# Two 16-head attentions: the diagonal corrections directly behind their scores, and two PSUM evictions per batch on ACT

## The chip, the cores and the metric

The kernel runs on one core of a Trainium2 chip. The metric is the time of one execution on the device in microseconds; a kernel's time is the median of its runs. A profile is one further execution, recorded by the hardware profiler. Names in it: PE is TensorE (matmuls), PEld its weight loads, DVE is VectorE, ACT is ScalarE, POOL is GpSimd, SP is SyncE, which issues DMAs here.

## The reference, cut to what matters

Four blocks follow each other on `x` of shape (8, 512, 128), each with a residual addition and a LayerNorm: an attention (layer 0), a feed-forward with FP4 quantization, a second attention (layer 1), and two layers of local attention with a feed-forward. The change touches the two 16-head attentions alone. Layer 0's adds a bias to the scores that falls with the distance of query and key (ALiBi); layer 1's has none.

```python
slopes = jnp.power(2.0, 8.0 * jnp.arange(0, -H, -1, dtype=jnp.float32) / H)
qkv = x @ W_qkv.T + b_qkv                       # B=8, S=512, H=16 heads of 8
...
scores = jnp.einsum('bhqd,bhkd->bhqk', q, k) / math.sqrt(Hd)
rel = jnp.abs(pos[None, :] - pos[:, None]).astype(jnp.float32)
bias = -slopes[:, None, None] * rel             # layer 0 only
probs = jax.nn.softmax(scores + bias[None], axis=-1)
out = jnp.einsum('bhqk,bhkd->bhqd', probs, v)
...
return out @ W_out.T + b_out
```

## The kernel before, in words

**Two passes over the scores.** `attention` (from L121) forms each head's scores twice. The first pass (`s_ps`) has queries on the partitions and 512 keys along the row, and DVE takes each row's maximum from it (L239). The second pass (`t_ps`) has keys on the partitions and 512 queries along the row; its operands hold one row more, the maximum found before, so that it yields the scores already shifted. ACT turns them into exponentials `e` (L245), which PE multiplies with the values (`values`, tile `av`). A column of ones among the values gives the denominators.

**Corrections.** Layer 0's bias comes from extra rows in the products' operands. They give the right distance everywhere but in the two 64 x 64 blocks on the diagonal that belong to the 128 partitions of a tile. `corrected` (L199) repairs these with four small bf16 products per pair of tiles, `sel` as weights and `tri` as the moving operand, 64 columns each, accumulated into the same tile. Layer 1 has `alibi` False and no corrections.

**Units and steps.** A unit is a batch and a group of four heads, 32 units per layer, eight steps each. `step(u, i, v, k)` (L209) does the first pass of two heads for unit `u` and 128 queries, and the second pass of two heads for unit `v`, which is two units (`LAG` of 16 steps) behind. The two heads of a step lie on the upper and the lower half of the array's rows (`slice(64 * j, ...)`), so their products can run side by side. A layer has 256 steps with scores and 256 with shifted scores, 16 steps later.

**What sets the order.** The order on PE is written out by hand: `mm` and `tr` (L126, L127) keep the program's order, so that nearly all PE rows of the profile bear these two lines; they are told apart by their tiles. Between steps, `todo` inserts the rest at fixed steps (L306 to L331): the transposition of the maxima (`shift`, tile `m_ps`, behind odd steps), the value products (behind even steps), the division (`divide`, `o_ps`), and once per batch `begin_x` (transposed input, `xt_ps` to `xT`), two `begin_qk`, `begin_v`, `end_o` (transposed output, `ot_ps` to `oT`) and `end_y`. DVE, ACT and POOL run in the order that the planner gives them from the same program.

**Buffers.** PSUM's eight banks are split into three for `s_ps` (two are used per step), four that `t_ps` shares with every other product (`bank`), and one for `av`.

```python
p_s, p_t, p_av = pool("as", 3, space=PSUM), pool("at", 4, space=PSUM), pool("aav", 1, space=PSUM)
```

Of the kernel before, what the change touches and what calls it, by code (L numbers as in the profile page):

```python
# [40 lines left out]
def body(ctx, tc, x, consts, rows, wa0, wa1, acols, bo, wf, wqkv, wo, w1, w2, cols, b2r, qs, ks, out):  # L41
    nc = tc.nc
# [78 lines left out]
    def attention(li, alibi, qs_, ks_, late=None):  # L121
# [6 lines left out]
        with ExitStack() as st:  # L128
# [21 lines left out]
            def begin_x(b, h):  # L150
                ps = bank("xt_ps")
                for c in range(NT):
                    tr(ps[:, c * P : (c + 1) * P], xn[:, b * NT + c, :], ident)
                h["xT"] = work.tile([P, S], F32, tag="xT", name="xT", bufs=1)
                nc.vector.tensor_copy(h["xT"], ps)

            def begin_qk(b, h, n):
                ps = bank("qk_ps")
# [40 lines left out]
            def corrected(ps, lo, at, stop):  # L199

                for a in range(2):
                    for j in range(2):
                        r = slice(64 * j, 64 * j + 64)
                        mm(
                            ps[j][:, lo + 64 * a : lo + 64 * a + 64], lhsT=sel[r, a * P : (a + 1) * P],
                            rhs=tri[r, at : at + 64], start=False, stop=stop and a == 1, skip_group_check=True,
                        )

            def step(u, i, v, k):  # L209


                if u:
                    blk, pp = i // 2, i % 2
                    p, lo = 2 * u["g"] + pp, (i // 2) * P
                    q, kk = qs_[u["b"] % 2], ks_[u["b"] % 2]
                    ps = [p_s.tile([P, S], F32, tag="s", name="s_ps") for j in range(2)]
                    for j in range(2):
                        r = slice(64 * j, 64 * j + 63)
                        mm(
                            ps[j], lhsT=q[r, p, lo : lo + P], rhs=kk[r, p, :], start=True, stop=not alibi,  # L220
                            skip_group_check=True,
                        )
                if v:
                    vp, vlo = 2 * v["g"] + k % 2, (k // 2) * P
                    q, kk = qs_[v["b"] % 2], ks_[v["b"] % 2]
                    ts = [bank("t_ps") for j in range(2)]
                    for j in range(2):
                        r = slice(64 * j, 64 * j + 64)
                        mm(
                            ts[j], lhsT=kk[r, vp, vlo : vlo + P], rhs=q[r, vp, :], start=True, stop=not alibi,  # L230
                            skip_group_check=True,
                        )
                if u:
                    if alibi:
                        corrected(ps, lo, 0, True)
                    if i == 0:
                        u["m"] = work.tile([P, 2, 2, NT], F32, tag="m", name="m")
                    for j in range(2):
                        nc.vector.tensor_reduce(u["m"][:, j, pp, blk : blk + 1], ps[j], AX.X, ALU.max)  # L239
                if v:  # L240
                    if alibi:
                        corrected(ts, vlo, 64, True)
                    for j in range(2):
                        e = work.tile([P, S], F32, tag="e", name="e", bufs=13)
                        nc.scalar.activation(e, ts[j], AF.Exp, scale=float(SLOPES[2 * vp + j]) if alibi else 1.0)  # L245
                        v["e"].append(e)
# [43 lines left out]
            def end_o(h):  # L290
                ps = bank("ot_ps")
                for c in range(NT):
                    tr(ps[:, c * P : (c + 1) * P], h["o"][:, c, :], ident)
                h["oT"] = work.tile([P, S], F32, tag="oT", name="oT", bufs=1)
                nc.vector.tensor_copy(h["oT"], ps)

            def end_y(b, h):
                ps = bank("y_ps").rearrange("p (c d) -> p c d", c=NT)
# [11 lines left out]
            for n in range(B * G):  # L310
                b, g = divmod(n, G)
                units.append({"b": b, "g": g, "h": batch[b], "e": []})
                s, z = n * NU, n * NU + LAG
                later(s + 9, shift, units[n])
                later(z + 12, divide, units[n])
                for blk in range(NT):
                    later(z + 2 * blk + 4, values, units[n], blk)
                if g == 0 and b + 1 < B:

                    early = max(s - 10, 1)  # L320
                    later(early, begin_x, b + 1, batch[b + 1])
                    later(early + 2, begin_qk, b + 1, batch[b + 1], 0)
                    later(early + 4, begin_qk, b + 1, batch[b + 1], 1)
                    for part in range(2):
                        for j in range(2):
                            later(s + 6 + 12 * part + 2 * j, load_qk, b + 1, batch[b + 1], j, part)
                    later(s + 20, begin_v, b + 1, batch[b + 1])
                    later(s + 20, with_bias, b + 1)
                if g == G - 1:
                    later(z + 15, end_o, batch[b])  # L330
                    later(z + 18, end_y, b, batch[b])  # L331

            begin_x(0, batch[0])
            begin_qk(0, batch[0], 0)
            begin_qk(0, batch[0], 1)
# [4 lines left out]
            ps = bank("c_ps")[:, 0:P]  # L340
# [5 lines left out]
            for s in range(B * G * NU + LAG + 20):  # L346
                n, i = divmod(s, NU)
                m, k = divmod(s - LAG, NU)
                step(units[n] if n < B * G else None, i, units[m] if 0 <= m < B * G else None, k)
                for f, a in todo.pop(s, []):  # L350
                    f(*a)
# [562 lines left out]
```

## Time and profile before

| | us |
|---|---|
| median of three runs (2224.75 to 2230.90) | 2230.73 |
| the profiled execution's own time | 2234.28 |
| span of the profile, first to last instruction | 2232.5 |
| PE / PEld busy | 1784.9 / 985.4 |
| DVE busy | 1483.3 |
| ACT busy | 1156.5 |
| POOL busy | 830.6 |

Layer 0's attention lies at about 58 to 570 us of the span, the quantized feed-forward until about 763, layer 1's attention until about 1240, the rest belongs to the last block. A row of the page's fifth part reads: line, engine, operation, tile written, tile read, shape, count | busy us in total, mean ns of one | idle us of the engine just before such instructions, and what ended most of that idle time. In the timeline a line is: start in us, length in us, engine, line, operation, tiles, shape, count, and in brackets the idle time before it and its releaser. Several instructions of one kind close together are merged into one line.

### The profile page before, as it was taken

Reading aid. Unit: us, or ns where it says so; the run is one execution under the profiler, and the core shown is the slowest. Engines: PE = TensorE matmul, PEld = TensorE weight load, DVE = VectorE, ACT = ScalarE, POOL = GpSimd, SP = SyncE. Lnnn points to the kernel's source line nnn. Section 1 sums busy time; section 2 is a strip of 40 time slices with the busy share of each in tenths; the row PEclk is TensorE's granted clock in tenths of the full one; section 3 lists DMA queues with packets and bytes.
Section 4 is the critical chain, followed back from the end, with each engine's and each line's share of the span. In section 5 each row is a group of like instructions: output and inputs, shape, how many; then the busy total and the mean of one; then the engine's idle time right before and its main releaser. Section 6 shows DMA issues by size and latency. Waiting matters only on the chain.

```text
span 2232.5 us, 38302 instructions
## 1 busy us (share of the span) xinstructions
PE 1784.9 (80%) x14215; PEld 985.4 (44%) x14245; DVE 1483.3 (66%) x3156; ACT 1156.5 (52%) x2717; POOL 830.6 (37%) x880
## 2 busy tenths in 40 slices
PE   1899999999466589999999568788888888888884
PEld 0444444444244333333333235455555555555553
DVE  2677777776788368888886367566666666666662
ACT  0266666667222237777777145455555555555561
POOL 2302222212545521222211445444444444555554
PEclk6699999999678669999999779899999999999997
DMA  6522223210000132223210011111111111111110
GB/s 115 156 54 59 54 49 53 59 21 2 11 1 0 30 95 58 58 60 64 63 37 2 24 24 29 27 27 25 27 27 27 26 27 26 29 29 30 27 35 19
DMA packets 91627, 88.44 MB, mean 40 GB/s; under 512 B 45825, under 2 KB 57473, under 8 KB 91442
## 3 DMA queue, kind: packets, MB, share of 16 engines
q1 hardware_dynamic: 86752, 85.00, 17.3%
q8 instruction: 113, 1.85, 0.4%
q0 software_dynamic: 4096, 0.54, 0.2%
q14 instruction: 72, 0.59, 0.1%
q10 hardware_dynamic: 594, 0.47, 0.1%
HBM read 41.33 MB, written 18.87 MB: 27 GB/s over the span
## 4 chain that ended last, share of the span: by engine, by line
PE 29%; DVE 17%; ACT 13%; POOL 4%; issue 1%; DMA 1%; SPq 0%; ACTq 0%; POOLq 0%; DVEq 0%
ACT pw L463 7%; PE s_ps L126 6%; PE av L126 5%; PE qk_ps L461 4%; DVE t L564 3%; DVE r L560 3%; DVE m L239 3%; DVE ss L568 3%; DVE m L624 3%; ACT sq L463 2%; PE t_ps L126 2%; PE p_ps L462 2%; PE gp L461 1%; PE ap L461 1%; ACT L463 1%
## 5 line engine op out<-in xcount | busy, mean ns | idle before, releaser
L239 DVE TENSOR_REDUCE m<-s_ps 128x1 f32<-128x512 f32 x1024 | 647.4, 684 | 229.5 <-PE s_ps L126 120.6
L245 ACT ACTIVATE e<-t_ps 128x512 f32<-128x512 f32 x1024 | 552.9, 595 | 240.7 <-PE t_ps L126 236.1
L126 PE MATMUL s_ps<-k,q 63*128 63x512 f32 x1024 | 384.7, 511 | 108.5 <-DVE m L239 65.6
L126 PEld LDWEIGHTS s_ps<-k,q 63*128 63x128 f32 x1024 | 151.6, 192 | 401.3 <-DVE m L239 288.3
L463 ACT ACTIVATE pw<-sp,m,nrm 128x128 f32<-128x128 f32 x512 | 226.5, 461 | 153.0 <-DVE m L626 140.5
L126 PE MATMUL t_ps<-q,k 64*128 64x512 f32 x1024 | 286.2, 426 | 0.3 <-ACT e L245 0.2
L126 PE MATMUL av<-e,va 128*32 128x512 f32 x2048 | 275.2, 608 | 0.0
L257 POOL DMA_DIRECT2D q<-mt x128 | 68.4, 538 | 505.4 <-ACT mt L253 505.4
L571 POOL TENSOR_TENSOR r<-r,t 128x1024 f32<-128x1024 f32 x64 | 151.1, 2360 | 231.0 <-DVE t L564 221.6
L560 DVE TENSOR_TENSOR r<-qk_ps,tab 128x512 f32<-128x512 f32 x128 | 87.7, 685 | 160.6 <-ACT sq L463 160.6
L461 PE MATMUL qk_ps<-wqkv_s,hT 128*128 128x512 f32 x256 | 151.1, 721 | 45.8 <-ACT hT L464 30.3
L637 POOL TENSOR_TENSOR pw<-pw,den 128x1024 f32<-128x1024 f32 x64 | 121.4, 1897 | 137.4 <-DVE den L636 137.3
L126 PEld LDWEIGHTS t_ps<-q,k 64*128 64x128 f32 x1024 | 127.2, 188 | 16.7 <-ACT e L245 16.5
L463 ACT ACTIVATE sq<-qk_ps 128x1024 f32<-128x1024 f32 x64 | 67.2, 1050 | 94.9 <-PE qk_ps L461 89.7
L463 ACT ACTIVATION_READ_ACCUMULATOR pw<-sp,m,nrm 128x1 f32 x512 | 106.0, 207 | 0.0
L462 PE MATMUL p_ps<-cst,pw 128*128 128x128 f32 x512 | 77.9, 290 | 29.9 <-DVE pT L668 11.0
L668 DVE COPY pT<-p_ps 128x512 f32<-128x512 f32 x128 | 83.9, 686 | 23.7 <-PE p_ps L462 22.1
L461 PE MATMUL gp<-nT,w_s 128*128 128x512 f32 (+1 forms) x96 | 61.0, 722 | 45.4 <-ACT u L463 45.3
L462 PE MATMUL t_ps<-cst,r 128*128 128x128 f32 x512 | 78.2, 296 | 22.9 <-DVE xs L702 19.9
L564 DVE TENSOR_TENSOR t<-qk_ps,tab 128x256 f32<-128x256 f32 x256 | 95.3, 413 | 0.0
L461 PEld LDWEIGHTS qk_ps<-wqkv_s,hT 128*128 128x128 f32 x256 | 51.1, 222 | 95.0 <-issue 59.2
L126 PEld LDWEIGHTS <-sel 64*128 64x128 bf16 x2048 | 69.3, 97 | 52.1 <-issue 39.2
(161 smaller groups left out, 3208.5 us busy)
## 6 DMA issues: line engine op xcount, KB each, us to landing
far<-parts SPq DMA_DIRECT2D x64, 256.0 KB
q<-far SPq DMA_DIRECT2D x256, 64.0 KB
k<-far SPq DMA_DIRECT2D x256, 64.0 KB
ve<-v SPq DMA_DIRECT2D x112, 128.0 KB
xn<-in_x SPq DMA_DIRECT2D x8, 256.0 KB
q<-mt POOLq DMA_DIRECT2D x128, 4.0 KB, 2.9
hn<-xs SPq DMA_DIRECT2D x16, 128.0 KB
out<-xn SPq DMA_DIRECT2D x8, 256.0 KB
```

The source lines that it names most:

```text
L126: mm = lambda *a, **k: tc.keep_in_program_order(nc.tensor.matmul(*a, **k))
L239: nc.vector.tensor_reduce(u["m"][:, j, pp, blk : blk + 1], ps[j], AX.X, ALU.max)
L245: nc.scalar.activation(e, ts[j], AF.Exp, scale=float(SLOPES[2 * vp + j]) if alibi else 1.0)
L257: nc.gpsimd.dma_start(out=q[at : at + 1, 2 * g : 2 * g + 2, :].bitcast(F32).rearrange("o a (c t) -> o (a c) t", t=P), in_=mt[8 * j : 8 * j ...
L461: mm = lambda *a, **k: tc.keep_in_program_order(nc.tensor.matmul(*a, **k))
L462: tr = lambda *a, **k: tc.keep_in_program_order(nc.tensor.transpose(*a, **k))
L463: act = lambda *a, **k: tc.keep_in_program_order(nc.scalar.activation(*a, **k))
L560: nc.vector.tensor_tensor(heads(r[:, n]), heads(ps[:, n]), cos.unsqueeze(1).broadcast_to([P, HEADS, DH]), ALU.mult)
L564: nc.vector.tensor_tensor(heads(t2[:, n])[:, :, a : a + 32], heads(ps[:, n])[:, :, 32 - a : 64 - a], sin[:, a : a + 32].unsqueeze(1).broad ...
L571: nc.gpsimd.tensor_tensor(r, r, t2, ALU.add)
L637: nc.gpsimd.tensor_tensor(pw.rearrange("p s r k -> p (s r) k"), pw.rearrange("p s r k -> p (s r) k"), den.rearrange("p s r -> p (s r)").un ...
L668: nc.vector.tensor_copy(h["pT"][:, s], ps)
```

## The change

In `step`, the four corrections of the first pass are issued directly behind the two score products and ahead of the two shifted-score products; before, they stood behind those. The corrections of the second pass stay where they were. In `begin_x` and `end_o` the copies out of PSUM into `xT` and `oT` move from DVE to ACT: one each per batch and layer, 32 in all. On ACT each of them takes its place behind the exponentials of the step after which it is called.

```diff
@@ begin_x
                 h["xT"] = work.tile([P, S], F32, tag="xT", name="xT", bufs=1)
-                nc.vector.tensor_copy(h["xT"], ps)
+                nc.scalar.copy(h["xT"], ps)
@@ step
                             ps[j], lhsT=q[r, p, lo : lo + P], rhs=kk[r, p, :], start=True, stop=not alibi,
                             skip_group_check=True,
                         )
+                    if alibi:
+                        corrected(ps, lo, 0, True)
                 if v:
...
                 if u:
-                    if alibi:
-                        corrected(ps, lo, 0, True)
                     if i == 0:
                         u["m"] = work.tile([P, 2, 2, NT], F32, tag="m", name="m")
@@ end_o
                 h["oT"] = work.tile([P, S], F32, tag="oT", name="oT", bufs=1)
-                nc.vector.tensor_copy(h["oT"], ps)
+                nc.scalar.copy(h["oT"], ps)
```

## The prediction

> **What bounds the kernel now.** I read the page first, then the stretches of equal work, then the waits, then single steps in the timeline. The page puts the two attention layers' row of maxima at the top:
>
> ```profile
> L239 DVE TENSOR_REDUCE m<-s_ps 128x1 f32<-128x512 f32 x1024 | 647.4, 684 | 229.5 <-PE s_ps L126 120.6
> ```
>
> It is not saturated, though. In the stretch of layer 0 in which the granted clock is whole (98.9 to 546.8 us; columns: PE, PEld, DVE, ACT, POOL, clock, DMA share, GB/s) DVE is busy 335 of 448 us and ACT 289:
>
> ```profile
> 98.90:546.80 447.90, 411.71 (x4115) 203.71 (x4115) 335.48 (x604) 289.13 (x555) 91.83 (x128) 1.00 0.22 44
> ```
>
> So a loop of waits sets the pace. The waits from 160 to 540 us name it (total, times, longest): scores wait for a maximum, and the maximum waits for PE, in fact for the shifted scores' products.
>
> ```profile
> PEld s_ps L126 <- DVE m L239: 112.0, 156, 0.8
> ...
> DVE m L239 <- PE t_ps L126: 88.3, 187, 1.7
> ```
>
> In layer 1 (850 to 1160 us), which has no corrections, the same maximum waits for its own scores:
>
> ```profile
> DVE m L239 <- PE s_ps L126: 50.1, 85, 1.6
> ```
>
> The timeline of two steps of layer 0 shows the loop (start, length, engine, what):
>
> ```profile
> 301.80 0.50 PE L126 MATMUL s_ps<-k,q 63*128 63x512 f32 x2
> ...
> 302.14 0.40 PE L126 MATMUL t_ps<-q,k 64*128 64x512 f32 x2
> ...
> 302.38 0.23 PE L126 MATMUL s_ps<-tri,sel 64*128 64x64 bf16 x4
> 302.44 0.22 PE L126 MATMUL t_ps<-tri,sel 64*128 64x64 bf16 x4
> ...
> 302.65 1.29 DVE L239 TENSOR_REDUCE m<-s_ps 128x1 f32<-128x512 f32 x2 [0.54 <-PE t_ps L126]
> ...
> 303.40 0.50 PE L126 MATMUL s_ps<-k,q 63*128 63x512 f32 x1 [0.42 <-DVE m L239]
> ...
> 303.98 0.23 PE L126 MATMUL s_ps<-tri,sel 64*128 64x64 bf16 x2
> ...
> 304.20 1.06 PE L126 MATMUL av<-e,va 128*32 128x512 f32 x8
> 304.23 1.29 DVE L239 TENSOR_REDUCE m<-s_ps 128x1 f32<-128x512 f32 x2 [0.28 <-PE t_ps L126]
> ...
> 305.20 0.49 PE L126 MATMUL s_ps<-k,q 63*128 63x512 f32 x2
> ```
>
> Call the step at 301.80 X (odd) and the next Y (even, followed by the value products av). With three s_ps buffers and two per step, Y's second score needs the first maximum of X.
> - X to Y, 1.60 us, hangs on DVE: 0.58 until the first correction, 0.27 until the maximum starts, 0.69 for it, 0.06 until the score starts (303.40).
> - Y to the next X, 1.80 us, hangs on PE alone: score, shifted score, corrections, then av until 305.20. DVE's maximum that the next X needs would be done at 304.23 + 0.69 = 304.92.
>
> A pair takes 3.40 us.
>
> **What the Trainium skill says.** "TensorE: Matmul & The Clock Gate", section "Step-by-step: what each phase is for": a weight load is pulled ahead of running matmuls when the background weight buffer is free. The trace agrees: behind the long score, t_ps takes 0.24 us to its successor (302.14 to 302.38), while the score, whose load was held by the wait, takes 0.34. The same page, "Weight-path perf modes — Fast Weight Load (FWL) and DoubleRow", has faster loads for 128 weights that are not FP32: the trace has 97 ns for sel against 188 to 192 for t_ps and s_ps. Its section "The mechanism" says that matmuls start and end in program order. Starts here don't (a t_ps correction at 303.88, ahead of the s_ps ones at 303.98), but the maximum at 304.23 waited for the later, so ends are counted in order. "SBUF — State Buffer", "Who interferes with whom": ACT never waits for another engine's port; ACT's 0.59 us copy at 770.58 beside a busy POOL agrees.
>
> **Part 1: corrections behind their scores (layer 0 only).** Nothing is added or removed: four small products per step change places with the two shifted scores. No DMA moves, and POOL's and SP's orders stay as they were.
>
> *Gain, X to Y.* The corrections start 0.34 after the score instead of 0.58. The maximum starts at 0.34 + 0.27 = 0.61 instead of 0.85, Y's score at 0.61 + 0.69 + 0.06 = 1.36 instead of 1.60: 0.24 us saved. Layer 1 supports it: with no corrections its scores start at 1002.88, its maximum at 1003.41 while the t_ps products run, and its Y score at 1004.16, 1.28 later. PE has time: its own work in X would let Y begin at 0.70 to 0.80.
>
> *Loss.* t_ps now follows a short correction, so its weight load is no longer hidden. Layer 0's tail, where steps have no scores, shows that very order:
>
> ```profile
> 541.16 0.39 PE L126 MATMUL t_ps<-q,k 64*128 64x512 f32 x2
> 541.39 0.23 PE L126 MATMUL s_ps<-tri,sel 64*128 64x64 bf16 x4
> 541.46 0.22 PE L126 MATMUL t_ps<-tri,sel 64*128 64x64 bf16 x4
> 541.51 0.48 PE L126 MATMUL t_ps<-q,k 64*128 64x512 f32 x2
> 541.84 0.23 PE L126 MATMUL t_ps<-tri,sel 64*128 64x64 bf16 x4
> ```
>
> t_ps behind a score has 0.23 to 0.24 to its successor, behind a correction 0.33: 0.09 more. In X it falls into PE's wait for DVE (0.80 against 1.36) and costs nothing; if that cover went, it would be another 0.09. In Y it lies on the path: 1.80 becomes 1.89. Its bounds are 0 (the load hidden after all) and 0.24 (as much as the gain, if turning to and fro between bf16 and f32 costs more than the tail shows); I take 0.09.
>
> *Sum.* A plain pair gains 0.24 - 0.09 = 0.15. From step 21 (97.4 us, clock whole) to 254 there are 117 pairs. Seven hold ot_ps in X (0.59 us more of PE, 285.27 to 285.86): there PE reaches Y at 0.80 + 0.67 = 1.47, so 0.1 is saved and 0.09 lost, nothing. 110 x 0.15 = 16.5. Steps 16 to 20 are at half clock and PE-bound: 5 x 0.1 = 0.5 lost. The 16 steps before have no t_ps, the 16 behind no scores. Layer 0: **16.0 us**.
>
> ACT's exponentials come later by the 0.09 and sooner with the pair; ACT would be busy (289 + 8) of 432 us, 69% instead of 65%. Y's second t_ps needs, in steps with m_ps or ot_ps, the bank of X's first exponential: free at about 1.09 + 0.60 + 0.06 = 1.75, wanted at 1.36 + 0.41 = 1.77. That cover is thin, and a miss of 0.05 in the 36 pairs concerned would cost 2 us.
>
> **Part 2: 32 copies of 0.69 us from DVE to ACT, 0.59 there (rows of L193 and L272).** Off DVE in layer 0: xT at 284.58 ends ahead of the maximum at 285.33; oT at 286.53 delays Y's maxima by 0.23, which nobody on PE's path needs. So nothing is gained, but with the maximum due at 0.61 instead of 0.85, xT left on DVE would be late. In layer 1 xT at 1041.64 delays the maximum from 0.53 to 0.72 behind its scores: 6 x 0.15 = **1 us**, the ot_ps products capping it. On ACT, xT lies between Y's and X's exponentials, where ACT idles 1.3 us (285.47, 1042.29); oT lies behind X's and delays Y's by about 0.2, which the av products, using exponentials three steps old, don't feel. If it did hold the banks, it would be 0.2 x 13, under 3 us. At the start of layer 1 the xT copy took 1.69 us on DVE (763.19), beside other DVE and POOL work, and 14 us of loading follow from it; ACT would have it at about 763.9 instead of 764.9: **1 us** (0 to 1.1). Two tails 0.1 each: **0.2**. The first xT of layer 0 starts nothing that is late.
>
> Together 16.0 + 2.2 = **18 us**. The profiled execution took 2234.28 us (span 2232.5), 3.5 above the median of 2230.73; the gain is subtracted from the median: **2212 us**. A measurement of this kernel can tell about 0.3%, 6.7 us.
>
> **Rivals.**
> - *The load is free* (0 instead of 0.09): 0.24 x 110 + 2.2 = 28.6, 2202. Against it: the tail's 0.33. Chance 0.1.
> - *The gain is eaten:* the reload, or banks held by ACT, costs about 0.2 per pair: 110 x 0.04 + 2 = 6, 2224 to 2230. For it: the thin bank margin. Chance 0.11.
> - *Slower:* the maximum does not start sooner, its release still tied to the t_ps pair. Then X to Y grows by 0.09 and Y to X by 0.09: 110 x 0.18 - 2 = +18, 2249. It decides from a maximum starting later than about 0.78 behind its scores (0.85 - 0.09 + the 0.02 of part 2). For it: the page's releaser is t_ps. Against it: layer 1's start at 0.53 with t_ps still running. Chance 0.07.
> - *The order is not as written* (the planner moves the corrections back): the built order has the four corrections between the pairs in every step, so next to no chance.
>
> The forecast keeps 0.71. Range 2202 to 2225, from the free load to most of the gain eaten. Faster by over 0.3% (below 2224): the forecast and the free load, 0.82; within it 0.11, slower 0.07.
>
> **What would show it.** Right: "DVE m <- PE t_ps" gone from the waits, "<- PE s_ps" in its place; maximum 0.61 behind the scores, Y's score 1.36, next X 1.89 later; pair 3.25; t_ps to its correction 0.33; layer 1's step pair still 2.93. Wrong: the maximum at 0.8 or later, Y to X above 2.04 (the whole 0.24 lost), PE waiting for exponentials ahead of t_ps, or DVE gaps behind ACT's copies.

## The result, and the profile after

The changed kernel takes **2208.93 us** (median of four runs, 2201.63 to 2214.46) against 2230.57 (four runs): by the medians 21.6 us less. The ratio of the runs is given as 0.9915 with a 95% interval of 0.9889 to 0.9940, about 19 us (13 to 25); it is not the quotient of the two medians, which is 0.9903. The profiled execution took 2210.63 us with a span of 2208.9; the one before took 2234.28 and 2232.5.

The page's row of the maxima has the same busy time as before and names the scores for nearly all of its idle time, 241.8 us instead of 120.6 (before, another 108.4 of its 229.5 us stood behind the shifted scores' products):

```profile
L239 DVE TENSOR_REDUCE m<-s_ps 128x1 f32<-128x512 f32 x1024 | 647.9, 685 | 247.2 <-PE s_ps L126 241.8
```

The waits of layer 0 from 160 to 520 us say where that comes from (engine and line, what it waited for, us in total, times, longest). The maximum now waits for its own scores' products, and the scores' weight loads wait for the maximum 76 us instead of 112 in the slightly longer window shown before. No wait of a maximum for t_ps is left.

```profile
ACT e L245 <- PE t_ps L126: 87.7, 160, 1.4
DVE m L239 <- PE s_ps L126: 76.8, 104, 1.8
PEld s_ps L126 <- DVE m L239: 76.2, 131, 0.8
```

The timeline of one pair of steps shows why. X has its scores at 259.55, Y its second score at 260.90.

```profile
259.55 0.49 PE L126 MATMUL s_ps<-k,q 63*128 63x512 f32 x2
...
259.89 0.23 PE L126 MATMUL s_ps<-tri,sel 64*128 64x64 bf16 x4
...
259.96 0.48 PE L126 MATMUL t_ps<-q,k 64*128 64x512 f32 x2
260.16 2.63 DVE L239 TENSOR_REDUCE m<-s_ps 128x1 f32<-128x512 f32 x4 [0.71 <-PE s_ps L126]
...
260.28 0.23 PE L126 MATMUL t_ps<-tri,sel 64*128 64x64 bf16 x4
...
260.90 0.18 PEld L126 LDWEIGHTS s_ps<-k,q 63*128 63x128 f32 x1 [0.40 <-DVE m L239]
...
261.80 1.07 PE L126 MATMUL av<-e,va 128*32 128x512 f32 x8
...
262.80 0.50 PE L126 MATMUL s_ps<-k,q 63*128 63x512 f32 x2
```

The maximum starts at 260.16, 0.61 behind the scores and while t_ps is still running. Y's second score follows at 260.90, 1.35 behind them. The next X is at 262.80, another 1.90 later. t_ps has 0.32 us to its correction (259.96 to 260.28). It is so throughout: in the median of the 81 plain ones of layer 0 the maximum starts 0.61 behind the first score, 0.85 before the change, and Y's first score 0.80 behind X's instead of 0.70.

The stretch from step 21 to the last scores, called the steady stretch below, before (97.4 to 540.8) and after, in the columns of the earlier stage line:

```profile
97.40:540.80 443.40, 407.25 (x4070) 202.07 (x4069) 334.29 (x602) 284.92 (x545) 90.69 (x126) 1.00 0.22 45
```

```profile
97.60:525.80 428.20, 421.02 (x4070) 203.78 (x4069) 327.43 (x589) 291.25 (x558) 90.62 (x126) 1.00 0.23 46
```

PE has the same 4070 products, and the stretch is 15.2 us shorter. PE's busy time rises by 13.8 us all the same, so it is no measure of the work here. Thirteen copies have left DVE (602 to 589 instructions) and come to ACT (545 to 558).

Where the time went, from the starts of the first and last scores and of layer 1's first xT copy in each trace:

| stretch, us | before | after |
|---|---|---|
| start to first scores, to step 21 | 36.5 + 60.9 | 37.3 + 60.3 |
| layer 0, step 21 to the last scores | 443.4 | 428.3 |
| to layer 1's xT copy (quantized feed-forward) | 222.4 | 221.1 |
| xT copy to layer 1's first scores | 22.0 | 20.2 |
| to step 21, to the last scores | 36.1 + 393.2 | 35.0 + 392.5 |
| the rest (the last block) | 1018.0 | 1014.3 |

The last block's code is untouched. In all profiles of this study it takes between 1008.2 and 1018.0 us, so its 3.7 us here are not put down to the change. The stretch up to layer 1's xT copy lies between 221.0 and 224.5 in the kernels of this study, and layer 1's first 21 steps take 35.2 us in the corrections-only kernel, whose code for layer 1 is that of the kernel before; so neither of these two differences is shown to be the change's.

### The profile page after: what moved, and what is told of

Read it like the earlier page. It is cut to its first block, busy times and chain, and to the rows that moved or that the text cites. A ratio compares the mean times of both kernels' runs of the same rounds, so it can differ in the third digit from the quotient of the medians.

```text
span 2208.9 us, 38298 instructions
## 1 busy us (share of the span) xinstructions
PE 1788.6 (81%) x14215; PEld 982.2 (44%) x14245; DVE 1467.8 (66%) x3124; ACT 1171.9 (53%) x2749; POOL 829.8 (38%) x880
## 4 chain that ended last, share of the span: by engine, by line
PE 28%; DVE 17%; ACT 13%; POOL 4%; issue 2%; DMA 1%; SPq 0%; ACTq 0%; POOLq 0%; DVEq 0%
ACT pw L463 7%; PE s_ps L126 6%; PE av L126 6%; PE qk_ps L461 4%; DVE t L564 3%; DVE r L560 3%; DVE m L239 3%; DVE ss L568 3%; DVE m L624 2%; ACT sq L463 2%; PE t_ps L126 2%; PE p_ps L462 2%; PE gp L461 1%; PE ap L461 1%; ACT L463 1%
## 5 line engine op out<-in xcount | busy, mean ns | idle before, releaser
L239 DVE TENSOR_REDUCE m<-s_ps 128x1 f32<-128x512 f32 x1024 | 647.9, 685 | 247.2 <-PE s_ps L126 241.8
L126 PE MATMUL s_ps<-k,q 63*128 63x512 f32 x1024 | 373.9, 510 | 78.4 <-DVE m L239 31.8
L126 PE MATMUL t_ps<-q,k 64*128 64x512 f32 x1024 | 301.8, 452 | 0.3 <-ACT e L245 0.2
L126 PEld LDWEIGHTS t_ps<-q,k 64*128 64x128 f32 x1024 | 135.5, 189 | 16.7 <-ACT e L245 16.4
L126 PEld LDWEIGHTS <-sel 64*128 64x128 bf16 x2048 | 83.4, 97 | 72.4 <-issue 41.9
L668 DVE COPY pT<-p_ps 128x512 f32<-128x512 f32 x128 | 84.0, 687 | 21.6 <-PE p_ps L462 19.9
```

The costliest lines, as they stand in the source:

```text
L126: mm = lambda *a, **k: tc.keep_in_program_order(nc.tensor.matmul(*a, **k))
L668: nc.vector.tensor_copy(h["pT"][:, s], ps)
```

## The experiments

Each kernel starts from the changed one, or from the one before, as said. Numbers per pair are medians of the time between the starts of the second scores of successive steps, worked out from the traces, between step 21 and step 254; "X to Y" runs from an odd step to the even one, "Y to X" from there to the next odd step. Of the 117 pairs 29 have the m_ps product behind X and 7 the ot_ps products; the other 81 are the plain ones.

| layer 0, X to Y + Y to X, us | plain | m_ps in X | ot_ps in X | step 21 to last scores |
|---|---|---|---|---|
| before | 1.59 + 1.80 | 1.59 + 1.80 | 1.59 + 2.85 | 443.4 |
| changed | 1.35 + 1.89 | 1.35 + 1.89 | 1.48 + 2.95 | 428.3 |
| corrections only | 1.35 + 1.89 | 1.35 + 1.89 | 1.48 + 2.95 | 428.1 |
| load covered | 1.35 + 2.02 | 1.35 + 2.09 | 1.60 + 3.08 | 446.3 |
| 16 products more in X | 1.35 + 1.89 | 1.35 + 2.09 | 1.70 + 2.94 | 435.1 |
| 16 products more in Y | 1.35 + 2.12 | 1.35 + 2.12 | 1.47 + 3.18 | 455.0 |
| shifted scores first, k = 0, 4, 6 | 1.36 + 1.50 | 1.36 + 1.89 | 2.13 + 2.54 | 398.5 |
| shifted scores first in all even steps | 1.35 + 1.50 | 2.12 + 1.48 | 2.12 + 2.54 | 408.8 |

**Corrections only.** The changed kernel with its copies back on DVE:

```diff
-                nc.scalar.copy(h["xT"], ps)
+                nc.vector.tensor_copy(h["xT"], ps)
...
-                nc.scalar.copy(h["oT"], ps)
+                nc.vector.tensor_copy(h["oT"], ps)
```

> The corrections moved as in the change, the copies into xT and oT left on DVE. Theory (the loop score - maximum - next score is shortened by 0.24 us per pair of steps, a weight load of 0.09 is uncovered): layer 0 keeps nearly all its gain, 14 to 16 us; in the seven pairs with xT the copy now ends after the maximum could start and takes back 0.1 to 0.15 each; layer 1 is as before. Time 2213 to 2217. Rival (the gain comes from relieving DVE of 32 copies of 0.69 us): little or nothing is left, 2226 to 2231.

Measured: 2213.24 us, ratio to before 0.9915 (0.9901 to 0.9929), no different from the whole change. Layer 0 keeps all of its gain. The corrections carry the gain that these times can tell; the rival that the copies carry it falls. One expectation failed: xT on DVE was to take back 0.1 to 0.15 in seven pairs. There are six such pairs in the steady stretch, and it cost 0.10 in one of them and nothing in five. The timeline of one of the five shows the copy in the way and the maximum at 276.82, 0.72 instead of 0.61 behind the scores of 276.10:

```profile
276.21 0.69 DVE L155 COPY xT<-xt_ps 128x512 f32<-128x512 f32 x1 [0.71 <-PE xt_ps L127]
276.82 1.28 DVE L239 TENSOR_REDUCE m<-s_ps 128x1 f32<-128x512 f32 x2
```

But these five X steps also hold the ot_ps products, and PE reaches Y at 1.47 to 1.48 anyway. The sixth, step 23, holds none: there Y follows at 1.45 instead of the changed kernel's 1.35.

**Copies only.** The kernel before with the two copies on ACT (the same lines, the other way round).

> The 32 copies on ACT as in the change, the corrections left where they were. Theory: layer 0's pairs stay at 1.60 + 1.80 us; layer 1 gains about 1 in six pairs with xT and 1 to 2 at its start, where the DVE copy took 1.69 us: 2226 to 2229. Rival (the copies carry the gain): 2209 to 2214. The sum of this run's and the other half's gains should be that of the change, 21.6, within 3.

Measured: 2223.47 us, ratio 0.9973 (0.9959 to 0.9988): by the ratio 6 us less (the medians are 7.6 apart). It lies below the 2226 to 2229 that were expected. Its trace finds 0.4 us in layer 0 (443.0) and 1.0 us in layer 1 from step 21 on (392.2). At layer 1's start the copy of 1.69 us becomes one of 0.58. The first line is the kernel before, the second this one:

```profile
763.19 1.69 DVE L155 COPY xT<-xt_ps 128x512 f32<-128x512 f32 x1
```

```profile
761.89 0.58 ACT L155 COPY xT<-xt_ps 128x512 f32<-128x512 f32 x1 [0.41 <-ACT xn L112]
```

The way from there to the first scores is 19.8 us instead of 22.0, but with the copy on DVE the corrections-only kernel has 20.7, and the kernels with it on ACT lie between 18.3 and 20.4; so about 1 us is put down to the copy, which is shorter by that much, and the rest to the loading's own spread. That leaves 2 to 3 us that the trace can place; for the rest of the 6 it shows no place but the first steps of the layers and the last block, which vary as much without a change. The two halves' gains were to add up to 21.6 within 3. They come to 0.85% and 0.27%, together 1.12% or 25 us, a little over 3 too much and just past the upper end of the whole change's interval (0.60 to 1.11%). The halves' own intervals (0.71 to 0.99% and 0.12 to 0.41%) leave room for a plain sum. But corrections alone and the whole change have the same ratio, so what the copies add in time lies between nothing and some 6 us and is not settled; only the traces place 2 to 3.

**The load covered.** In layer 0 a product with zeros opens each t_ps bank behind the corrections of s_ps, and the shifted scores accumulate onto it (calls set on one line here and below):

```diff
+                    if alibi:
+                        for j in range(2):
+                            r = slice(64 * j, 64 * j + 64)
+                            mm(ts[j], lhsT=sel[r, 0:P], rhs=zero[r], start=True, stop=False, skip_group_check=True)
...
-                            ts[j], lhsT=kk[r, vp, vlo : vlo + P], rhs=q[r, vp, :], start=True, stop=not alibi,
+                            ts[j], lhsT=kk[r, vp, vlo : vlo + P], rhs=q[r, vp, :], start=not alibi, stop=not alibi,
```

> Layer 0 only: a product of sel with zeros, 512 columns, opens each t_ps bank ahead of the shifted scores, which accumulate onto it, so a long bf16 product stands between the corrections and the shifted scores. Theory (the 0.09 us is the weight load of t_ps, uncovered behind a short product): t_ps to its correction falls from 0.33 to 0.24 us; the added product costs 0.22 to 0.24 on the path in Y and nothing in X, so Y to X is about 2.04 and layer 0 is 15 to 20 us longer. Rival (the 0.09 is the price of turning from bf16 to f32 operands): t_ps to its correction stays 0.33, and Y to X is 2.13.

Measured: 2219.91 us in one run; layer 0 is 18.0 us longer than the changed kernel's. The quantity that was named cannot be read: the shifted scores start 0.03 behind the zeros in the trace, so a start there is not the moment at which a product streams.

```profile
262.36 0.38 PE L126 MATMUL t_ps<-zero,sel 64*128 64x512 bf16 x2
262.39 0.58 PE L126 MATMUL t_ps<-q,k 64*128 64x512 f32 x2
262.81 0.23 PE L126 MATMUL t_ps<-tri,sel 64*128 64x64 bf16 x4
```

What can be read is both together: 0.45 us (262.36 to 262.81) for two products of 512 columns. That is twice 0.22 to 0.24. With the 0.33 of an uncovered load 0.12 would be left for the zeros, half of what such a product takes. Y to X is 2.02, as the weight load predicts (2.04), and not 2.13. So the 0.09 fits a load that is hidden by a long product ahead of it and not by a short one; a fixed price for turning from bf16 to f32 is against the sum. The load itself was not measured apart; the reading rests on these sums.

**Sixteen products more in X, or in Y.** Small products of sel with zeros, accumulated into t_ps ahead of its corrections, in the odd or the even steps of layer 0:

```diff
+            def nothing_added(ps, lo):
+                for _ in range(4):
+                    for a in range(2):
+                        for j in range(2):
+                            r = slice(64 * j, 64 * j + 64)
+                            mm(ps[j][:, lo + 64 * a : lo + 64 * a + 64], lhsT=sel[r, a * P : (a + 1) * P],
+                               rhs=zero[r], start=False, stop=False, skip_group_check=True)
...
                     if alibi:
+                        if k % 2 == 1:          # X; 0 in the other kernel, for Y
+                            nothing_added(ts, vlo)
                         corrected(ts, vlo, 64, True)
```

> The changed kernel with 16 more small products per odd step X of layer 0 (sel times zeros, eight per half of the array, ahead of the corrections of t_ps). Theory: they take about 0.25 us and fall into PE's wait for DVE's maximum (0.80 + 0.25 against 1.36): X to Y stays 1.35 in plain pairs, 1.48 + 0.25 in the seven with ot_ps. X's exponentials come 0.25 later, so in the 29 pairs with m_ps Y's second t_ps waits for its bank (1.06 + 0.25 + 0.66 = 1.97 against 1.77): 0.2 each. Layer 0 in all 6 to 9 us longer than the change's. Rival (PE is the bound throughout): 120 x 0.25 = 30 us longer.

> The same 16 products in the even steps Y. Theory (Y to X is PE alone): Y to X grows from 1.89 to about 2.14 in every pair, X to Y stays 1.35: layer 0 about 117 x 0.25 = 29 us longer than the change's. Rival (DVE or ACT bounds Y to X): less than 10 us.

Measured: 2214.45 and 2231.13 us in one run each; layer 0 is 6.8 us longer with the products in X and 26.7 with them in Y. In X plain pairs do not feel them at all: PE waits there for the maximum. The 6.8 us lie where they were expected, in ot_ps pairs (1.48 to 1.70) and, by 0.20, in those with m_ps. These lines of the X kernel show the bank: the exponentials of 253.86 end their first at 254.45, and only then Y's second t_ps can begin (at 254.51), so that its correction, and with it av, comes late (255.01 where the scores began at 253.90).

```profile
253.69 0.28 PE L127 MATMUL m_ps<-cst,m 128*16 128x128 f32 x1
253.86 1.09 ACT L260 ACTIVATE e<-t_ps 128x512 f32<-128x512 f32 x2 [1.05 <-PE t_ps L126]
...
254.31 0.69 PE L126 MATMUL t_ps<-q,k 64*128 64x512 f32 x2
...
255.01 1.06 PE L126 MATMUL av<-e,va 128*32 128x512 f32 x8
```

In Y every pair pays 0.23. So X to Y is DVE's, Y to X is PE's, and the bank's margin is real but not used up by the change: 0.25 us more cost 0.20, so about 0.05 was left.

**Shifted scores first in even steps.** If PE idles ahead of Y's second score and is the bound behind it, the shifted scores belong in the gap. In outline (k = 2 is left out because its X holds m_ps):

```diff
+                first = v and k in (0, 4, 6)
+                if first:
+                    shifted_scores()      # the two t_ps products and their corrections
+                if u:
+                    scores()              # the two s_ps products and their corrections
+                if v and not first:
+                    shifted_scores()
```

> In the even steps Y with k = 0, 4, 6 the shifted scores and their corrections go ahead of the scores, in both layers; all else is as in the changed kernel. Theory (X to Y waits for DVE's maximum with PE idle, Y to X is PE alone): the shifted scores fill the wait, so Y to X falls by about 0.33 (0.24 and the uncovered load) to 1.56 in layer 0 and by about 0.25 in layer 1, X to Y stays 1.36 and 1.28: three pairs of four, less the seven and six pairs with the ot_ps products, where the bank of X's first exponential is late (0.4 each): 80 x 0.33 + 80 x 0.25 - 5 = 41 us less, about 2168. Rival A (DVE is the bound already in Y to X): the time stays near 2209. Rival B (the shifted scores in front wait for ACT to free a bank, and the scores queue behind them): slower than 2209, with PE waits for e ahead of t_ps.

Measured: **2158.88 us**, ratio to before 0.9672 (0.9656 to 0.9688). X to Y stays 1.36, Y to X falls to 1.50 in layer 0 and from 1.67 to 1.43 in layer 1. That is 50 us below the changed kernel; 41 were expected. The expectation counted 0.33 per plain pair of layer 0, the product and its load, and 0.39 were found: the product's corrections moved as well, about 0.07 by an estimate from the changed kernel's timeline, where such corrections stand 0.07 apart from the next product (259.89 to 259.96). Of a plain pair, from X's scores to the next X's:

```profile
259.20 0.50 PE L126 MATMUL s_ps<-k,q 63*128 63x512 f32 x2
...
260.00 0.48 PE L126 MATMUL t_ps<-q,k 64*128 64x512 f32 x2
260.32 0.23 PE L126 MATMUL t_ps<-tri,sel 64*128 64x64 bf16 x4
260.39 0.67 PE L126 MATMUL s_ps<-k,q 63*128 63x512 f32 x2
260.71 0.42 PE L126 MATMUL s_ps<-tri,sel 64*128 64x64 bf16 x4
261.06 1.07 PE L126 MATMUL av<-e,va 128*32 128x512 f32 x8
```

Y's t_ps at 260.00 runs while DVE takes X's maxima, and av starts 0.35 us behind Y's first correction. DVE is now close to the bound: four maxima of 2.62 us in a pair of 2.86, with 0.24 idle between them.

```profile
279.61 2.62 DVE L254 TENSOR_REDUCE m<-s_ps 128x1 f32<-128x512 f32 x4 [0.24 <-PE s_ps L126]
282.46 2.62 DVE L254 TENSOR_REDUCE m<-s_ps 128x1 f32<-128x512 f32 x4 [0.24 <-PE s_ps L126]
```

The steps left out of this order were tested by taking them in:

```diff
-                first = v and k in (0, 4, 6)
+                first = v and k % 2 == 0
```

> As the shifted-first kernel, but with k = 2 as well, whose X holds m_ps. Theory (Y's shifted scores wait there for the bank of X's first exponential, and the scores queue behind them): X to Y rises from 1.35 to about 1.8 in those pairs, Y to X falls from 1.89 to 1.50, so the pair is the same within 0.1 and the time within 5 us of 2159. Rival (no bank wait): these pairs gain 0.39 and 0.24 too, 29 x 0.63 = 18 us less.

Measured: 2177.24 us in one run, 18 us more, not within 5. The mechanism is the one named, its size was not: X to Y becomes 2.12, not 1.8. The timeline has Y's second t_ps waiting for the bank until 257.39, 1.71 behind the scores of 255.68, and the second score follows it only at 257.80, since it has to wait for that product and its corrections as well.

```profile
257.39 0.18 PEld L126 LDWEIGHTS t_ps<-q,k 64*128 64x128 f32 x1 [0.42 <-ACT e L258]
...
257.80 0.47 PE L126 MATMUL s_ps<-k,q 63*128 63x512 f32 x1
```

**Shifted scores first, spared behind ot_ps.**

```diff
-                first = v and k in (0, 4, 6)
+                first = v and (k in (4, 6) or k == 0 and v["g"] != 1)
```

> As the shifted-first kernel (k = 0, 4, 6), but with the scores first again in the even steps whose X holds the ot_ps products (first step of the second group of heads). Theory: these pairs go back from 4.67 to about 4.43 us in layer 0 and from 4.14 to 3.99 in layer 1, 7 x 0.24 + 7 x 0.15 = 2.7 us less, 2156. Rival (their time is lost to the copies on ACT in either order): no change, 2159.

Measured: 2158.59 us, ratio 0.9685 (0.9649 to 0.9721). In the trace the pairs with ot_ps go back to 1.48 + 2.95 as expected, worth 1.3 us in layer 0 (397.2) and 1.0 in layer 1 (374.1 instead of 375.1), 2.3 where 2.7 were expected. The times cannot tell so little apart: either version beats both kernels by 50 to 72 us.

## Why the prediction was right

The forecast was 2212 us, 18 less than before; measured were 2208.93 and 21.6 by the medians, about 19 by the ratio, whose interval reaches from 13 to 25 us. The traces place 17 of it: 15.1 in layer 0's steady stretch, 0.7 in layer 1's and about 1 at layer 1's start. What the total has beyond that lies in stretches that vary as much without a change, so how near the total came says less than the terms below.

- *X to Y, 1.60 to 1.36.* Measured 1.59 to 1.35. The maximum starts 0.61 behind the scores as said. The slower rival, a release tied to the t_ps pair, falls with that line. (Its ground was put down to the page's releaser; the page names the scores, and it is the list of waits that names t_ps.)
- *Y to X, 1.80 to 1.89.* Measured 1.80 to 1.89, in every plain pair. The 0.09 was taken from layer 0's tail, where the same order of products already stood in the trace before. That it is the weight load is supported by the load-covered kernel. The rival of a free load falls, and so does that of an eaten gain.
- *The sum of layer 0, 16.0 us.* Measured 15.1 from step 21 to the last scores. A plain pair gains 0.14 to 0.15 (3.39 to 3.24). The pairs with ot_ps were put at nothing and gained 0.01. The half-us loss while the clock is low is not to be seen: the first 21 steps took 60.9 and 60.3, and between 57.6 and 60.9 in all kernels here.
- *ACT and its banks.* Priced as a thin margin that might cost up to 2 us. The products added in X show what it is worth: 0.25 us later exponentials cost 0.20 in each pair with m_ps. The change's 0.09 stayed inside: pairs with m_ps and plain ones are alike.
- *The copies, 2.2 us.* The 1 us in layer 1's steps was there (0.7 in the changed kernel, 1.0 in the copies-only one): in each of the six pairs with xT, X to Y falls from 1.45 to 1.28, 0.17 where 0.15 was put. The ot_ps products do not cap it. At the start 1 us from copy to projection is seen: PE begins the projections at 747.59, 1.09 behind the end of ACT's last xn (746.50); before it was 765.06, 2.16 behind 762.90. The corrections-only kernel, with the copy on DVE, keeps the longer way: 2.17. The first scores gained 1.8, of which the rest is put down to the loading's spread. The term was undersized if the copies-only time is taken at its word: 6 us there (3 to 9) against 2.2, of which the traces place 2 to 3.
- *A reason that was wrong.* "xT left on DVE would be late": in the corrections-only kernel it is late by 0.11 us, but of the six X steps that hold it in the steady stretch five hold the ot_ps products too, and it costs nothing there; it costs 0.10 in the one that doesn't.

The profiled runs differ by 23.6 us, of which 3.7 are the last block's; no step of the prediction speaks of that block. The chances of the outcomes add up to 0.99, a slip that changes nothing.

## What to carry to other kernels

When an engine in order feeds a loop through a second engine, put what the loop waits for ahead of everything that doesn't hurry, and price what the new neighbours do to each other: here the order uncovered a weight load, and a corner of the old trace where the same neighbours stood gave its price. Then look at which half of the loop has the idle time. The larger gain lay in moving the unhurried products into the other engine's wait. In the pairs with m_ps or ot_ps it was limited by a PSUM bank that ACT frees late, in the plain pairs DVE is nearly full; whether more banks would give more was not tried.

## What the runs showed of the hardware

- An f32 product with 128 weights takes 0.23 to 0.24 us to its successor behind a product of 512 columns on the same half of the array (302.14 to 302.38 and 541.16 to 541.39 before), and 0.32 to 0.33 behind one of 64 (541.51 to 541.84 before, 259.96 to 260.28 after). The 0.09 fits a weight load that only the long product hides.
- A product's start in the trace can come 0.03 us behind that of a 512-column product ahead of it on the same half (262.36 and 262.39 in the load-covered kernel), so it is not the moment at which the product streams. Sums over a chain of products can be read, single lengths cannot.
- The "idle before" of a group can hide a wait. The steady stretch of layer 0 has 33.7 us of s_ps idle behind maxima before the change and 0.8 after it, although each Y still waits: its weight load shows 0.40 us in the timeline above and 90.0 us in all, after 132.1. Now a product on the other half of the array counts PE as busy nearly all of that time:

```profile
L126 PE MATMUL s_ps<-k,q 63*128 63x512 f32 x468 | 171.3, 494 | 36.2 <-DVE m L239 33.7
```

```profile
L126 PE MATMUL s_ps<-k,q 63*128 63x512 f32 x468 | 162.8, 494 | 7.2 <-DVE m L239 0.8
```
